# Values in matmuls of 128 patches: a change of lanes in a gated convolution before a GRU scan

## The chip, the cores and the metric

The kernel runs on one core of one Trainium2 chip. The metric is the device time of one execution in microseconds. The engines are TensorE (PE, with its weight loads as PEld), VectorE (DVE), ScalarE (ACT), GpSimd (POOL) and SyncE (SP, which only issues DMAs here). All tensors are float32.

## The reference

Two layers, each with a residual and a group norm in front. Only layer 0 bears on the change. Its input is x, 4 images of 64 channels, 256 x 256 pixels.

```python
hidden = jnp.einsum('bchw,oc->bohw', x, w1)                 # 64 -> 384 channels
hidden = jax.lax.conv_general_dilated(hidden, w_dw, ...)    # 3 x 3, each channel by itself
q, k, v = jnp.split(hidden, 3, axis=1)                      # 128 channels each
qf = jnp.fft.rfft2(_to_patches(q))                          # patches of 8 x 8 pixels
kf = jnp.fft.rfft2(_to_patches(k))
out = jnp.fft.irfft2(qf * kf, s=(P, P))
...
mu = out.mean(axis=1, keepdims=True)                        # over the 128 channels, per pixel
var = out.var(axis=1, keepdims=True)
out = (out - mu) / jnp.sqrt(var + 1e-05) * ln_w[None, :, None, None] + ln_b[None, :, None, None]
out = v * out
return jnp.einsum('bchw,oc->bohw', out, w_out)              # 128 -> 64 channels
```

Layer 1 is a scan of a GRU cell over the 256 columns of the result.

## The kernel before

**Blocks.** Layer 0 runs over NBLK = 32 blocks, each of 128 patches (NP = 128, in two halves of NJ = 64) with all channels. The patches come with a halo, as 100 numbers (10 x 10). In a block:

- Chunk 0, 1 and 2: `pointwise` (line 358) for 16 units of 4 patches in each half. A unit is 8 matmuls into two banks of PSUM, and one copy into `h`, which holds 100 halo pixels on its lanes, and 128 channels by 128 patches along each lane. Most copies are ScalarE's; those of a few units are VectorE's (the last argument). Chunk 0 and 1 bring the first and the second half of q and k, chunk 2 brings v.
- `circular` (line 404), after chunk 0 and again after chunk 1: for sp = 0 to 3, `transform` multiplies `h` by matrices that hold the 3 x 3 taps and the Fourier transform (streamed from DRAM as `t`), ScalarE copies q, VectorE multiplies k by q twice (`products`), POOL adds (`crossed`). `inverse` (line 419) transforms a pair back, 24 matmuls, and ScalarE copies the result into `z`. Four pairs give the 128 channels. An inverse is put off in `pending` and issued by `flush`.
- After chunk 2: `project` for the second half of the block before, then `values` (line 441): for k = 0 to 7, 16 channels each, 32 matmuls with the taps alone, and `keep_values`, which copies to `v`.

**Layout.** `z` and `v` are [128, NJ, E]: the lane is the half of the patches and the pixel (2 x 64), and along it lie 64 patches by 128 channels. The order of the channels is `channel_of`'s.

**The norm and what follows** is a generator, `layer_norm` (line 460), and each call of `go()` issues its next step on VectorE. Its steps in order: statistics of channels 0 to 63 (32 `bn_stats`, in four steps, beside circular(n, 1)), of channels 64 to 127 (16 + 16, after units 6 and 7 of chunk 2), a step with the small instructions on mean and variance and the first of eight passes over `z` (subtract the mean or multiply by the reciprocal deviation, 32 channels at a time), the seven other passes, then eight transposes in blocks of 32 x 32, of `z` and `v` in turn. After them the channels lie on lanes. `gated` (line 515) scales and shifts `z` on ScalarE and multiplies `v` by it on POOL, for 32 channels a call. `project` (line 539) is 32 matmuls of 512 columns into four banks: each row tile of the array has its own bank. `add_residual` (line 556) adds x from the four banks with four VectorE instructions, `leave` takes statistics and writes `x1`.

**Order.** Every instruction goes through `InOrder`, so each engine runs its own in the program's order. The norm of block n runs while block n + 1 is computed: the passes and transposes beside its chunk 0, `gated` beside circular(n + 1, 0), `project` and `add_residual` of u = 0 after unit 11 of chunk 1 and of u = 1 after chunk 2. The last stands like this (lines 685 to 689):

```python
            po = project(n - 1, 1) if n else None
            go(1)
            if n:
                add_residual(1, po, xr[1])
            go(3)
```

**Banks.** PSUM is one ring of eight banks, and `psum` (line 283) hands them out in the order of the calls; a call for four starts at bank 0 or 4. Who is given a bank again waits until its last reader is done.

```python
        def psum(banks=2):
            at = place[0] + (-place[0]) % banks
            place[0] = (at + banks) % 8
            return ring[:, at % 8 : at % 8 + banks]
```

Of the kernel before, what the change touches and what calls it, by code (L numbers as in the profile page):

```python
# [9 lines left out]
F32 = mybir.dt.float32  # L10
# [7 lines left out]
E = 2 * C  # L18
P = 128
# [16 lines left out]
def channel_of(f):  # L36

    pair, rest = divmod(f, 32)
    c, r = divmod(rest, 8)
    t, s = divmod(r, 4)  # L40
    return (2 * pair + t) * 16 + 4 * s + c
# [121 lines left out]
def tile_conv_then_gru(  # L163
# [47 lines left out]
    with tc.tile_pool(name="xa", bufs=5) as xa, tc.tile_pool(name="sta", bufs=1) as sta, tc.tile_pool(  # L211
# [55 lines left out]
        wo_sb = const.tile([P, 4, C], F32, tag="wo", name="wo_sb")  # L267
        nc.sync.dma_start(wo_sb, w_out.rearrange("a f b c -> (a f) b c"))
        ln_sb = const.tile([P, 2, 4], F32, tag="ln", name="ln_sb")
# [6 lines left out]
    with layer0 as s:  # L276
# [13 lines left out]
        z = big.tile([P, NJ, E], F32, tag="z", name="z")  # L290
        v = big.tile([P, NJ, E], F32, tag="v", name="v")
        wk = big.tile([P, 7, 1024], F32, tag="wk", name="wk")
        lnst = big.tile([P, 512], F32, tag="lnst", name="lnst")
        seen = big.tile([P, 1024], F32, tag="seen", name="seen")
        moments = big.tile([P, 2, NJ], F32, tag="moments", name="moments")
# [39 lines left out]
        def unit_of(n, chunk, unit, vector):  # L335
# [5 lines left out]
            for j in range(4):  # L341
# [12 lines left out]
                h.rearrange("p c (g n) -> p g c n", g=2)[:, :, c0:c1, unit * 4 : unit * 4 + 4],  # L354
# [64 lines left out]
        def inverse(n, pair):  # L419

            pz = psum(4)
            for i in range(2):
                slot = PAIRS[pair % 2][i]
                both = wk[:, slot : slot + 2].rearrange("p t (r s g n) -> p r g t s n", r=2, g=2, n=NJ)
                for part in range(2 - i):
                    for g in range(2):
                        for c in range(4):
                            at = slice(32 * c, 32 * c + 32)
                            nc.tensor.matmul(
                                pz[g * 64 : g * 64 + 64, c].rearrange("p (t s n) -> p t s n", t=2, n=NJ),  # L430
                                lhsT=g_sb[at, part, i, :],
                                rhs=both[at, part, g],
                                start=i == part == 0,
                                stop=i == 1,
                                tile_position=(32 * c, g * 64),
                            )
            nc.scalar.copy(
                z[:, :, 32 * pair : 32 * pair + 32], pz.rearrange("p c (f n) -> p n (c f)", n=NJ)
            )

        def values(n, k, pv):

            m = matrix(n, 2, k)
            for f in range(16):
                for g in range(2):
                    nc.tensor.matmul(
                        pv[g * 64 : g * 64 + 64, f // 8, (f % 8) * NJ : (f % 8) * NJ + NJ],
                        lhsT=m[0:HALO, f, :],
                        rhs=h[:, 16 * k + f, g * NJ : g * NJ + NJ],
                        start=True,  # L450
                        stop=True,
                        tile_position=(0, g * 64),
                    )

        def keep_values(k, count, pv):
            nc.scalar.copy(
                v[:, :, 16 * k : 16 * (k + count)], pv.rearrange("p x (f n) -> p n (x f)", n=NJ)
            )

        def layer_norm(n):  # L460

            st = lnst[:, 0:384].rearrange("p (a i k) -> p a i k", a=2, k=6)
            spare = lnst[:, 384:512].rearrange("p (a n) -> p a n", a=2)
            mean, rstd = moments[:, 0], moments[:, 1]

            def statistics(a, p0, p1):

                for p in range(p0, p1):
                    nc.vector.bn_stats(
                        st[:, a, p, :],  # L470
                        z[:, 2 * p : 2 * p + 2, 64 * a : 64 * a + 64].rearrange("p n f -> p f n"),
                    )

            for i in range(4):
                statistics(0, 8 * i, 8 * i + 8)
                yield
            statistics(1, 0, 16)
            yield
            statistics(1, 16, NJ // 2)
            yield  # L480
            by = st.rearrange("p a i (e k) -> p a (i e) k", e=2)
            d, total = spare[:, 0], spare[:, 1]
            nc.vector.tensor_tensor(d, by[:, 0, :, 1], by[:, 1, :, 1], ALU.subtract)
            nc.vector.tensor_tensor(total, by[:, 0, :, 2], by[:, 1, :, 2], ALU.add)
            nc.vector.tensor_tensor(d, d, d, ALU.mult)
            nc.vector.scalar_tensor_tensor(d, d, 32.0, total, ALU.mult, ALU.add)
            nc.scalar.activation(rstd, d, AF.Sqrt, bias=eps, scale=1.0 / E)
            nc.vector.tensor_tensor(mean, by[:, 0, :, 1], by[:, 1, :, 1], ALU.add)
            nc.vector.tensor_scalar(mean, mean, 0.5, None, ALU.mult)
            nc.vector.reciprocal(rstd, rstd)  # L490

            def scaled(i):
                f = slice(32 * i, 32 * i + 32)
                for part, what in ((mean, ALU.subtract), (rstd, ALU.mult)):
                    nc.vector.tensor_tensor(
                        z[:, :, f],
                        z[:, :, f],
                        part.rearrange("p (n x) -> p n x", x=1).to_broadcast([P, NJ, 32]),
# [4 lines left out]
            def turned(of, i):  # L503
                chunk = of[:, :, 32 * i : 32 * i + 32]
                nc.vector.transpose(chunk, chunk)

            for i in range(4):
                yield from scaled(i)
            for i in range(4):
                turned(z, i)  # L510
                yield
                turned(v, i)
                yield

        def gated(n, i):
            f = slice(32 * i, 32 * i + 32)
            nc.scalar.activation(
                z[:, :, f],
                z[:, :, f],
                AF.Identity,  # L520
                bias=ln_sb[:, 1, i : i + 1],
                scale=ln_sb[:, 0, i : i + 1],
            )
            nc.gpsimd.tensor_tensor(v[:, :, f], v[:, :, f], z[:, :, f], ALU.mult)
# [14 lines left out]
        def project(n, u):  # L539
            po = psum(4)  # L540
# [415 lines left out]
```

## Time and profile before

| what | value |
|---|---|
| runs of the kernel before | 5211.36, 5244.66 and 5206.85 us, median 5211.36 |
| the profiled execution | 5232.48 us, span of the core 5230.5 us |
| granted TensorE clock, mean | 0.991 |
| moved by DMA | 785.06 MB, mean 150 GB/s |
| `values`: 16384 matmul records of 64 columns | 509.6 us busy, 35.3 us of waits before them |
| `bn_stats` of the norm | 2048, 416.6 us busy |
| passes over z | 256, 2278 ns each |
| transposes of z and of v | 128 each, 2293 and 2288 ns |
| ScalarE's copies of z, and of v | 128 at 1866 ns, 160 at 1521 ns in the mean |
| POOL's product of `gated` | 128 at 4556 ns |

One matmul of the program is two records in the profile[...]. In the rows of the profile the columns are: start and length in microseconds, engine, line, operation, what it writes and reads, and how many; in brackets the idle time of the engine before it, and what ended that. Nearly all rows have line 157, the helper that keeps the order, so a row is told by its tiles: `psring` is the ring of PSUM banks, `psring<-h,t` with 64 columns are the values, `psring<-v,wo_sb` is `project`. In the windows a row gives, for each engine, busy time and count, then the granted clock of TensorE (1.00 is full speed), the DMA share, and GB/s.

### The profile page before, as it was taken

How to read it: one execution, taken by the hardware profiler on the slowest of the kernel's cores; microseconds unless marked ns; L12 is line 12 of the kernel's file. 1: busy time of each engine (PE TensorE's matmuls, PEld its weight loads, DVE VectorE, ACT ScalarE, POOL GpSimd, SP SyncE). 2: the span in 40 equal slices, each digit the busy share in tenths (PEclk: the TensorE clock that was granted, in tenths of full speed). 3: DMA queues.
4: the chain of work that ended last, by engine and by line, in shares of the span. 5: the costliest groups of instructions: out<-in, count | busy, mean ns of one | idle time of the engine just before them, and what ended most of it. 6: DMA issues, size and time to landing. Idle time of an engine off the chain costs nothing.

```text
span 5230.5 us, 284031 instructions
## 1 busy us (share of the span) xinstructions
PE 4908.2 (94%) x131172; PEld 4285.8 (82%) x131172; DVE 4046.2 (77%) x7000; ACT 3325.4 (64%) x4253; POOL 1729.3 (33%) x1723
## 2 busy tenths in 40 slices
PE   4999999999999999999999999999699999999999
PEld 3888888788888888878887888888489999999998
DVE  4678888878788877888887777887677777777777
ACT  3666666666666666666666666676366666666665
POOL 0233332333323343333333323224243333333332
PEclk9999999999999999999999999999899999999999
DMA  7566766666666666666666556556443333333332
GB/s 264 147 168 173 187 175 167 169 174 175 176 183 179 168 170 170 174 182 174 171 171 158 148 157 167 163 150 162 108 118 99 98 98 100 99 97 98 99 99 66
DMA packets 421206, 785.06 MB, mean 150 GB/s; under 512 B 32604, under 2 KB 295552, under 8 KB 417632
## 3 DMA queue, kind: packets, MB, share of 16 engines
q1 hardware_dynamic: 366464, 533.76, 37.9%
q0 software_dynamic: 53264, 232.55, 15.2%
q8 instruction: 1027, 16.83, 1.4%
q14 instruction: 163, 1.34, 0.1%
q10 hardware_dynamic: 288, 0.58, 0.0%
HBM read 622.72 MB, written 144.05 MB: 147 GB/s over the span
## 4 chain that ended last, share of the span: by engine, by line
PE 82%; issue 6%; ACT 5%; DVE 4%; DMA 3%; POOL 1%; ACTq 0%; POOLq 0%; SPq 0%; DVEq 0%
PE psring L157 56%; PE pshz L157 8%; PE pshr L157 8%; PE psni L157 6%; DMA t<-t_all 2%; PE pshn L157 2%; ACT v L157 1%; DVE wk L157 1%; ACT z L157 1%; ACT xq L157 1%; DVE z L157 1%; DMA seen<-in_x 1%; DVE bn L157 0%; POOL v L157 0%; ACT h L157 0%
## 5 line engine op out<-in xcount | busy, mean ns | idle before, releaser
L157 PEld LDWEIGHTS psring<-h,t 100*32 100x32 f32 x49152 | 1387.6, 120 | 250.7 <-issue 198.0
L157 PE MATMUL psring<-h,t 100*32 100x128 f32 x49152 | 1468.2, 257 | 98.4 <-issue 63.2
L157 PEld LDWEIGHTS psring<-w_sb,xq 64*100 64x100 f32 x24576 | 1366.9, 164 | 126.4 <-issue 92.7
L157 PE MATMUL psring<-w_sb,xq 64*100 64x128 f32 x24576 | 1424.7, 272 | 37.3 <-issue 24.2
L157 ACT COPY h<-psring 100x1024 f32<-100x1024 f32 (+2 forms) x1371 | 1234.4, 988 | 332.3 <-PE psring L157 331.1
L157 DVE TENSOR_TENSOR wk<-psring,wk 128x1024 f32<-128x1024 f32 (+1 forms) x768 | 759.3, 1037 | 475.4 <-PE psring L157 333.6
L157 POOL TENSOR_TENSOR v<-v,z 128x2048 f32<-128x2048 f32 x128 | 582.6, 4556 | 667.1 <-DVE wk L157 603.6
L157 DVE TENSOR_TENSOR z<-z,moments 128x2048 f32<-128x2048 f32 x256 | 577.9, 2278 | 2.3
L157 ACT ACTIVATE z<-pshz,b_rz 128x288 f32<-128x288 f32 (+7 forms) x510 | 242.1, 475 | 467.2 <-PE pshz L157 467.2
L157 POOL TENSOR_TENSOR wk<-wk 128x1024 f32<-128x1024 f32 x128 | 303.2, 2369 | 619.9 <-DVE wk L157 605.4
L157 POOL TENSOR_TENSOR raw<-raw,st 128x512 f32<-128x512 f32 x256 | 303.1, 1184 | 535.6 <-DVE st L157 401.7
L157 ACT COPY z<-psring 128x2048 f32<-128x2048 f32 x128 | 238.9, 1866 | 358.8 <-PE psring L157 269.0
L157 PE MATMUL pshr<-st,wi 64*64 64x144 f32 (+7 forms) x12240 | 435.4, 270 | 23.9 <-DVE st L157 13.9
L157 PE MATMUL pshz<-st,wi 64*64 64x144 f32 (+7 forms) x12240 | 435.9, 270 | 10.7 <-issue 9.1
L157 PE MATMUL psni<-st,wi 64*64 64x144 f32 (+7 forms) x12240 | 433.1, 270 | 6.0 <-issue 2.3
L157 DVE COPY h<-psring 100x1024 f32<-100x1024 f32 x229 | 277.1, 1213 | 198.7 <-PE psring L157 185.0
L157 ACT COPY wk<-psring 128x1024 f32<-128x1024 f32 x256 | 259.4, 1013 | 251.8 <-PE psring L157 221.1
L157 DVE SCALAR_TENSOR_TENSOR g<-z,xn 128x288 f32<-128x288 f32 (+7 forms) x510 | 225.7, 443 | 249.9 <-ACT z L157 247.3
L157 DVE BATCH_NORM_STATS2 lnst<-z 128x6 f32<-128x128 f32 x2048 | 416.6, 281 | 0.0
L157 PEld LDWEIGHTS psni<-st,wi 64*64 64x64 f32 x12240 | 366.5, 133 | 47.8 <-issue 10.5
L157 ACT COPY v<-psring 128x2048 f32<-128x2048 f32 (+1 forms) x160 | 243.3, 1521 | 253.9 <-PE psring L157 253.9
L157 PE MATMUL psring<-wk,g_sb 32*64 32x512 f32 x6144 | 383.5, 602 | 18.4 <-issue 15.4
(96 smaller groups left out, 6733.7 us busy)
## 6 DMA issues: line engine op xcount, KB each, us to landing
t<-t_all SPq DMA_DIRECT2D x768, 400.0 KB
xq<-in_xh POOLq DMA_DIRECT2D x128, 800.0 KB, 5.9
wk<-in_x SPq DMA_DIRECT2D x256, 256.0 KB
x<-wk POOLq DMA_DIRECT2D x256, 256.0 KB, 5.4
seen<-in_x POOLq DMA_DIRECT2D x96, 512.0 KB, 7.4
raw<-x SPq DMA_DIRECT2D x128, 256.0 KB
raw<-x SPq DMA_DIRECT2D x256, 128.0 KB
out<-raw SPq DMA_DIRECT2D x128, 256.0 KB
```

Of the source, the lines that this page charges most:

```text
L157: return self.tc.keep_in_program_order(got(*args, **kwargs))
```

## The change

The lanes of `z` and `v` become channel parity and pixel: `z` and `v` are [128, NP, C], with 128 patches by 64 channels along each lane, and two neighbouring channels stand on the two halves of the lanes.

- `values` issues 16 matmuls of 128 columns for each k instead of 32 of 64. `inverse` issues the same 24 matmuls, with the parity in place of the half. The copies to `z` and `v` are as large as before; a pair's copy writes 16 of 64 channels for all 128 patches.
- `layer_norm`: each lane has half of a pixel's channels. So there are 128 `bn_stats` of 64 columns for 64 of 128 columns, the small instructions are on 128 patches and not 64, and the two halves of the lanes are joined by a copy across and four more instructions.
- Passes, transposes and `gated` go over 64 patches by 32 channels; `gated(i)` has channels b and half u from i = 2b + u, where it had four groups of channels.
- `project(u, a)` is half of the former `project`, 16 matmuls. Two row tiles of the array now write one bank, so the order of row tiles and banks changes between a = 0 and a = 1, and a copy of one column on ScalarE stands between: it waits for the first half's last matmuls, and the second half waits for it.
- Places: gated 3 goes from circular(n, 0) to behind unit 3 of chunk 1; project(0, 0) behind unit 12, project(0, 1) and its add_residual behind unit 13, `leave` behind unit 15 (before: 11, 11, 13); project(1, 0) behind unit 14 of chunk 2, project(1, 1) behind unit 15. The copy of unit 11 of chunk 1 is VectorE's in place of that of unit 12.

```diff
-        z = big.tile([P, NJ, E], F32, tag="z", name="z")
-        v = big.tile([P, NJ, E], F32, tag="v", name="v")
+        z = big.tile([P, NP, C], F32, tag="z", name="z")
+        v = big.tile([P, NP, C], F32, tag="v", name="v")
...
             nc.scalar.copy(
-                z[:, :, 32 * pair : 32 * pair + 32], pz.rearrange("p c (f n) -> p n (c f)", n=NJ)
+                z[:, :, 16 * pair : 16 * pair + 16], pz.rearrange("p c (s n) -> p n (c s)", n=NP)
             )
...
             m = matrix(n, 2, k)
-            for f in range(16):
-                for g in range(2):
+            for j in range(8):
+                for e in range(2):
                     nc.tensor.matmul(
-                        pv[g * 64 : g * 64 + 64, f // 8, (f % 8) * NJ : (f % 8) * NJ + NJ],
-                        lhsT=m[0:HALO, f, :],
-                        rhs=h[:, 16 * k + f, g * NJ : g * NJ + NJ],
+                        pv[e * 64 : e * 64 + 64, j // 4, (j % 4) * NP : (j % 4) * NP + NP],
+                        lhsT=m[0:HALO, 2 * j + e, :],
+                        rhs=h[:, 16 * k + 2 * j + e, :],
...
             for i in range(4):
-                statistics(0, 8 * i, 8 * i + 8)
+                statistics(0, 16 * i, 16 * i + 16)
+                if i == 3:
+                    nc.vector.tensor_copy(own, by[:, :, 1:3])
                 yield
-            statistics(1, 0, 16)
-            yield
-            statistics(1, 16, NJ // 2)
-            yield
+            for i in range(2):
+                statistics(1, 32 * i, 32 * i + 32)
+                yield
...
+            nc.vector.tensor_tensor(own, own, by[:, :, 1:3], ALU.add)
+            nc.vector.scalar_tensor_tensor(d, d, -2.0, own[:, :, 0], ALU.mult, ALU.add)
+            nc.vector.tensor_tensor(d, d, d, ALU.mult)
+            nc.vector.scalar_tensor_tensor(rstd, d, 16.0, rstd, ALU.mult, ALU.add)
+            for e in range(2):
+                nc.vector.tensor_copy(other[64 * e : 64 * e + 64], own[64 - 64 * e : 128 - 64 * e])
+            nc.vector.tensor_tensor(apart, mean, other[:, :, 0], ALU.subtract)
+            nc.vector.tensor_tensor(own, own, other, ALU.add)
+            nc.vector.tensor_tensor(apart, apart, apart, ALU.mult)
+            nc.vector.scalar_tensor_tensor(rstd, apart, 8.0, rstd, ALU.mult, ALU.add)
+            nc.scalar.activation(rstd, rstd, AF.Sqrt, bias=eps, scale=1.0 / E)
+            nc.vector.tensor_scalar(mean, mean, 0.25, None, ALU.mult)
             nc.vector.reciprocal(rstd, rstd)
...
+        def project(u, a, po=None, first=[]):
+            po = psum(4) if po is None else po
+            y = v.rearrange("p n (b k) -> p b n k", k=32)
+            for b in range(2):
+                for e in range(2):
+                    for ph in range(2):
+                        for s in range(2):
+                            r, g = 2 * e + ph, a ^ e
+                            n0 = 64 * u + 32 * g + 16 * s
+                            i = nc.tensor.matmul(
+                                po[s * 64 : s * 64 + 64, 2 * g + ph].rearrange("p (n k) -> p n k", k=32),
+                                lhsT=wo_sb[32 * r : 32 * r + 32, b, :],
+                                rhs=y[32 * r : 32 * r + 32, b, n0 : n0 + 16],
+                                start=a == b == 0,
+                                stop=a == b == 1,
+                                tile_position=(32 * r, s * 64),
+                            )
+                            if a == 0 and b == 1:
+                                first.append(i)
+                            if a == 1 and b == 0 and first:
+                                behind(i, first.pop())
+            if a == 0:
+                turn = nc.scalar.copy(tick, eps)
+                while first:
+                    behind(turn, first.pop())
+                first.append(turn)
+            return po
...
-                if n and sp == 3:
-                    gated(n - 1, sp)
...
-                pointwise(n, 1, unit, unit in (7, 12))
-                if n and unit == 11:
-                    add_residual(0, project(n - 1, 0), xr[0])
+                pointwise(n, 1, unit, unit in (7, 11))
+                if n and unit == 3:
+                    gated(n - 1, 3)
+                if n and unit == 12:
+                    po = project(0, 0)
                 if n and unit == 13:
+                    add_residual(0, project(0, 1, po), xr[0])
+                if n and unit == 15:
                     leave(n - 1, 0, xr[0])
...
+                if n and unit == 14:
+                    po = project(1, 0)
                 if unit % 4 == 3 and n + 1 < NBLK:
                     load(n + 1, unit // 4)
-            po = project(n - 1, 1) if n else None
+            if n:
+                project(1, 1, po)
             go(1)
             if n:
                 add_residual(1, po, xr[1])
```

## The prediction

> **What bounds the kernel now.** I read the engine totals first, then the chain that ended last, then the timeline of one block of layer 0 engine by engine.
>
> ```profile
> PE 4908.2 (94%) x131172; PEld 4285.8 (82%) x131172; DVE 4046.2 (77%) x7000; ACT 3325.4 (64%) x4253; POOL 1729.3 (33%) x1723
> PE 82%; issue 6%; ACT 5%; DVE 4%; DMA 3%; POOL 1%; ACTq 0%; POOLq 0%; SPq 0%; DVEq 0%
> ```
>
> TensorE is busy 94% of the span and 82% of the chain. So what this change is worth is read from TensorE: each microsecond it works less or waits more counts, and work of the others counts only where TensorE waits for it. Layer 1 (from about 3790 us on) is untouched. Layer 0 runs 32 blocks; by the starts of their first matmuls, blocks 2 to 30 take 113.3 us each in the mean (108.5 to 120.4). All numbers below are of block 12 (1462.7 to 1576.3 us) where nothing else is said. Its end on TensorE:
>
> ```profile
> 1546.73 8.98 PE L157 MATMUL psring<-w_sb,xq 64*100 64x128 f32 x160 [0.16 <-ACT z L157]
> 1555.64 3.69 PE L157 MATMUL psring<-v,wo_sb 32*64 32x512 f32 x64
> 1559.26 11.38 PE L157 MATMUL psring<-h,t 100*64 100x64 f32 x371
> 1572.02 4.31 PE L157 MATMUL psring<-h,t 100*64 100x64 f32 x141 [1.37 <-issue]
> ```
>
> The last pointwise units of chunk 2, project(1), then the values, without a pause between. And VectorE meanwhile:
>
> ```profile
> 1549.11 6.37 DVE L157 BATCH_NORM_STATS2 lnst<-z 128x6 f32<-128x128 f32 x32
> 1555.83 1.22 DVE L157 COPY h<-psring 100x1024 f32<-100x1024 f32 x1 [0.35 <-PE psring L157]
> 1556.97 0.53 DVE L157 TENSOR_TENSOR lnst<-lnst 128x64 f32<-128x64 f32 x3
> 1557.53 0.22 DVE L157 SCALAR_TENSOR_TENSOR lnst<-lnst 128x64 f32<-128x64 f32 x1
> ...
> 1558.17 0.55 DVE L157 RECIPROCAL moments<-moments 128x64 f32<-128x64 f32 x1
> 1558.64 2.23 DVE L157 TENSOR_TENSOR z<-z,moments 128x2048 f32<-128x2048 f32 x1
> 1560.79 2.47 DVE L157 TENSOR_TENSOR wk<-psring,wk 128x512 f32<-128x512 f32 x4
> ```
>
> The reader is to see the order of this queue: statistics, the copy of unit 15, the norm's small instructions, the first pass over z, and only then add_residual(1), which empties the four banks of project(1). It ends at 1563.26, four microseconds after the values began. That is harmless now: project(1) sits in banks 4-7, and values k = 0 and 1 take banks 0-3.
>
> **The change, part by part** (per block; blocks 1 to 31 have all of it).
>
> *Values.* 512 records of 64 columns become 256 of 128. Unstalled, 141 records take 4.31 us, 30.6 ns each, 15.7 us in all. 128 columns over two tiles of the array: 8.98/160 = 56.1 ns (the pointwise row), so 14.4 us: -1.3. The Trainium skill, "TensorE: Matmul & The Clock Gate", section "Wait — 56ns, not 53.3ns?", gives about 2.5 ns of fixed cost for a matmul; 256 records less would by that be worth only 0.6 us. I take the rows. ScalarE takes part back: its copies of v and normalisations of xq start when k = 1 is done (1563.26) and the copy of k = 3 and 4, which frees the banks of k = 6, starts 5.92 us later (1569.18) and takes 1.86. With k = 0 and 1 in 3.6 us that is 3.6 + 5.9 + 1.9 = 11.4, where TensorE would be ready at 10.8. So -0.7 (-1.3 to 0).
>
> *Banks.* The ring hands out banks in order of calls. project(1, 0) is now called one unit earlier, before unit 15. By the allocation rule in psum() it gets banks 0-3, unit 15 gets 4-5, and the next call for four banks, values k = 0, rounds up to 0-3 again: those of project(1). So the values now wait for add_residual(1), bank by bank, and that stands in VectorE's queue behind the norm and the first pass over z. This is the largest term.
>
> *The norm on VectorE.* bn_stats of 128 columns follow each other at 199 ns (6.37/32), of 512 at about 0.6 us (2.46 us for four); that gives 0.13 us for 64. The 64 in units 6 and 7 take 8.3 us, +1.9, about what unit 15 comes later (half of project, 1.85), so they hide. Behind unit 15's copy the small instructions take 1.67 us now (1556.97 to 1558.64). Then: five of 128 columns at about 0.23 (0.19 for 64, from 0.56 us for three, and 1.04 ns a column), 1.15; two of 256 at 0.39, 0.78; two copies across half the lanes at 0.25 to 0.39, 0.6; from the last one over ScalarE's square root to the reciprocal 0.64 now, 0.76; the reciprocal 0.47 now, and 64 columns more at 6.3 ns (553 ns for 64 columns, 177 for 4), 0.87. Sum 4.2 us.
>
> *The gate.* From TensorE's end of unit 15: 1.33 to the small instructions, 4.2 for them, 2.15 for the first pass (1558.64 to 1560.79), 0.7 for the first add: the values start after 8.4 us. From the same point project and nothing else took 3.62. Now half of project lies ahead of unit 15: 1.85 + 8.4 - 3.62 = +6.6 (5.5 to 7.5, as the small instructions take 3.2 to 5 us). The second half of project covers 1.85 of the 8.4, so TensorE stands idle for 6.5 us.
>
> *The clock.* A long pause costs more than itself here. At 253.00 TensorE paused for 3.12 us; after it:
>
> ```profile
> 253.00:256.20 3.20, 0.08 (x3) 0.08 (x2) 0.00 (x0) 0.90 (x1) 3.20 (x1) 1.00 0.99 169
> 256.20:259.60 3.40, 3.40 (x32) 3.40 (x34) 0.00 (x0) 1.18 (x2) 3.40 (x2) 0.50 0.29 100
> 259.60:263.00 3.40, 3.40 (x67) 3.40 (x64) 2.42 (x3) 2.50 (x3) 0.13 (x1) 1.00 0.00 0
> ```
>
> (busy time and count of PE first, the granted clock third from the end: 0.50, and 32 matmuls where the next 3.4 us hold 67.) So 1.7 us are lost. The same page, section "HAM oscillation — how this bites in real kernels", puts it as a rule that TensorE must not idle for more than about 3.4 us, and describes a loop that pays at every turn. The trace has too few such pauses for "at every turn"; without the rule this term could be 0, with it 1.7 to 3.4 (two stretches). I take +1.7.
>
> *z's copy in circular(n, 0).* A pair's copy now writes 16 channels of all 128 patches, so the first overlaps what gated 0 and gated 1 read; before it met gated 0 alone. POOL and ScalarE in the next block:
>
> ```profile
> 1605.32 4.60 POOL L157 TENSOR_TENSOR v<-v,z 128x2048 f32<-128x2048 f32 x1
> ...
> 1606.68 1.86 ACT L157 COPY z<-psring 128x2048 f32<-128x2048 f32 x1 [2.42 <-PE psring L157]
> 1608.60 1.01 ACT L157 COPY wk<-psring 128x1024 f32<-128x1024 f32 x1
> ```
>
> gated 1 ends at 1609.92, so z's copy slips by 3.2 us (median over the blocks 3.1), and behind it on ScalarE the copy of q for sp = 3, for which VectorE's products wait, and the copies of h. Moving gated 3 to unit 3 of chunk 1 takes 2.1 us of ScalarE out of that queue, and puts it where two later units may wait for copies. Following the banks: unit 0 of chunk 1 waits about 1.1 us for z's banks, unit 3 about 0.8 for the late products. +2.0 (0 to 2.5).
>
> *Statistics in circular(n, 1).* 4 x 16 instead of 4 x 8 at 0.13: +0.5 us at each step of VectorE, where it has 0.5 to 2.8 us of idle time; TensorE waited there for crossed and products already (0.91, 0.46). +0.5 (0 to 1.2).
>
> *project in two halves with a copy of one column on ScalarE between.* Same 64 records. The copy needs some 0.3 us (the sqrt of 64 columns takes 0.35), a pointwise unit of 0.9 us lies between the halves: hidden in both places; without that unit it would be about 0.5. Unit 15 of chunk 1 waits for the first two adds, +0.4, where before the inverse waited 0.2. project(0) no longer needs gated 3: TensorE waited 2.1 us in all for this row in layer 0, so nothing. The inverse has the same 24 matmuls: nothing. DMAs are as many; leave(0) is two units later, but its writes to x1 wait for the adds, not for this place.
>
> *What becomes free.* From the first matmul of the values to the first of the next block it is 16.67 us in the mean of blocks 2 to 30, where 15.72 is the least: TensorE lost 0.95, partly to weights that had not landed; a pause in front lets them land: -0.5. VectorE was late for units 3 and 9 of chunk 0 by about 0.4; TensorE now comes later: -0.4.
>
> Sum: -0.7 + 6.6 + 1.7 + 2.0 + 0.5 + 0.2 - 0.9 = +9.4 us, 31 times 291 us. The profiled execution took 5232, the median of the runs is 5211, 21 lower; blocks are as many in both, so the sum goes onto the median: about 5500.
>
> **The rivals.**
>
> *Gate without the rest.* If the clock holds, z's copy is hidden and the small instructions take 3.2 us, 4.6 a block remain: about 5355. Against it: the pause is still over 3.4 us.
>
> *VectorE as the bound, no gate.* From 1549 to 1615 VectorE idles for 2.5 us; 1.9 of statistics and 2.5 of small instructions make it longer by 2 us: 31 x 2 = 62, about 5275. It holds only if the values don't wait for project's banks.
>
> *Faster.* If the chain on VectorE were done in 1.9 us after unit 15 (it takes 1.33 before its first small instruction), the values would start as before and shorten: 31 x 0.7 to 1.3, 5170 to 5190. It decides by where add_residual(1) stands against the first pass over z, and the order is written down: behind it.
>
> *The change does less than it says:* TensorE could need as long for 128 columns as for two times 64. That would add 1.3 x 31 = 40 to any of these.
>
> **How the numbers follow.** The gate with clock and z's copy: 0.84, 5500, by its own bounds 5390 to 5610. The gate alone: 0.08. VectorE's bound: 0.03. No net difference: 0.02. Faster: 0.03. 1% of 5211 is 52 us, about what a measurement tells from no change; VectorE's bound lies on its edge and counts half for each side. Slower 0.94, same 0.03, faster 0.03. The range goes from 5375, which takes in part of the gate alone, to 5605.
>
> **What would show it.** Right: in the PE timeline a pause of 5 to 7 us before the values in each of the blocks 1 to 31, released by DVE wk; the values' row at x8192, about 450 us without the pauses; granted clock near 0.97 with a stretch of 0.5 after each pause; the first z copy of a block waiting for POOL v. Wrong: no pause ahead of the values (then the banks are not as I count them), a pause without a drop of the clock (then 5440), ScalarE's z copy not later than before (5430).

## The result, and the profile after

The changed kernel takes 5626.01 us in the median of 6 runs (5619.83 to 5633.22); the kernel before, run beside it, 5217.79 (6 runs). The ratio is 1.0769, with a 95% interval from 1.0746 to 1.0792. The forecast was 5500, with a range from 5375 to 5605: slower, as said, but by 408 us where the sum had 291, and 21 us above the top of the range.

The profiled execution took 5633.22 us, its span is 5631.4, its mean TensorE clock 0.966 (before 0.991). First the engine totals and the chain that ended last, from its page:

```profile
PE 5032.4 (89%) x122980; PEld 4370.6 (78%) x122980; DVE 4273.6 (76%) x9240; ACT 3347.3 (59%) x4317; POOL 1730.6 (31%) x1723
PE 65%; DVE 11%; ACT 8%; issue 7%; DMA 5%; POOL 3%; POOLq 0%; DVEq 0%; ACTq 0%; SPq 0%
```

TensorE had 82% of the chain and has 65% now; VectorE has 11% of it and ScalarE 8%. Who waits for whom is in the summary of waits (total us, times, longest), first of the kernel before:

```profile
PE psring L157 <- DVE wk L157: 2.9, 5, 1.2
```

and of the changed one:

```profile
PE psring L156 <- DVE wk L156: 237.5, 63, 7.4
```

`DVE wk` is VectorE writing `wk`, which is the add of the residual or a product of `circular`. The pauses ahead of the values, 31 of 7.0 us, make some 217 of the 237.5. The timeline of block 12 at its end, TensorE (start, length, what, count, in brackets the idle time before and its releaser):

```profile
1702.18 6.36 PE L156 MATMUL psring<-w_sb,xq 64*100 64x128 f32 x112 [0.96 <-DVE h L156]
1708.47 2.45 PE L156 MATMUL psring<-v,wo_sb 32*64 32x512 f32 x32
1710.86 1.12 PE L156 MATMUL psring<-w_sb,xq 64*100 64x128 f32 x16
1711.91 1.97 PE L156 MATMUL psring<-v,wo_sb 32*64 32x512 f32 x32
1720.89 7.76 PE L156 MATMUL psring<-h,t 100*64 100x128 f32 x96 [7.01 <-DVE wk L156]
1728.87 5.46 PE L156 MATMUL psring<-h,t 100*64 100x128 f32 x96 [0.22 <-ACT v L156]
```

and VectorE in the same stretch:

```profile
1699.36 1.29 DVE L156 BATCH_NORM_STATS2 bn<-seen 128x6 f32<-128x512 f32 x2 [4.75 <-DMA seen<-in_x]
...
1703.17 8.26 DVE L156 BATCH_NORM_STATS2 lnst<-z 128x6 f32<-128x64 f32 x64
1712.10 1.23 DVE L156 COPY h<-psring 100x1024 f32<-100x1024 f32 x1 [0.66 <-PE psring L156]
1713.24 0.42 DVE L156 TENSOR_TENSOR lnst<-lnst 128x256 f32<-128x256 f32 x1
1713.69 0.33 DVE L156 SCALAR_TENSOR_TENSOR lnst<-lnst 128x128 f32<-128x128 f32 x1
1714.05 0.33 DVE L156 TENSOR_TENSOR lnst<-lnst 128x128 f32<-128x128 f32 x1
...
1717.15 0.95 DVE L156 RECIPROCAL lnst<-lnst 128x128 f32<-128x128 f32 x1 [0.34 <-ACT lnst L156]
1718.02 2.23 DVE L156 TENSOR_TENSOR z<-z,lnst 128x2048 f32<-128x2048 f32 x1
1720.16 2.47 DVE L156 TENSOR_TENSOR wk<-psring,wk 128x512 f32<-128x512 f32 x4
```

and, in circular(n, 0) of the same block, POOL's product of gated 1 and ScalarE's first copy to z:

```profile
1640.11 4.54 POOL L156 TENSOR_TENSOR v<-v,z 128x2048 f32<-128x2048 f32 x1
1644.68 1.87 ACT L156 COPY z<-psring 128x2048 f32<-128x2048 f32 x1 [5.62 <-POOL v L156]
```

The reader is to see five things. The pause of 7.01 us stands where the prediction put it, and ends when the first add has read the first bank of project(1) (1720.16 plus 0.7). The first 96 records of the values take 7.76 us, the next 96 take 5.46: that is the half clock after the pause, as e3 below shows. The first half of project(1) takes 2.45, the second 1.97. VectorE stood 4.75 us at a count of the next image, waiting for its DMA. And z's copy stood 5.62 us, until gated 1 was done on POOL (2.42, for TensorE, before the change).

For the whole run, here are the stages of a block: microseconds between the first matmuls of stages, taken from the starts in the trace, as means of blocks 2 to 30. The last three columns are kernels of the experiments.

| stage | before | changed | e1 | e8 | e9 |
|---|---|---|---|---|---|
| chunk 0 | 15.28 | 14.87 | 19.24 | 15.15 | 15.15 |
| circular(n, 0) | 19.00 | 20.08 | 19.83 | 20.26 | 22.35 |
| chunk 1 with project(0) | 18.65 | 21.01 | 20.98 | 21.03 | 21.07 |
| circular(n, 1), 4 units of chunk 2, inverse | 28.10 | 28.09 | 28.22 | 28.48 | 28.33 |
| 12 units of chunk 2, project(1), pause | 15.62 | 24.97 | 18.43 | 18.45 | 17.14 |
| values | 16.67 | 17.74 | 17.93 | 17.89 | 15.67 |
| a block | 113.3 | 126.8 | 124.6 | 121.3 | 119.7 |

So the change costs 13.5 us a block, not 9.4. What the values save is there, but hidden under the clock; two stages bring what the prediction did not have: chunk 1 with project(0), and chunk 2.

### The profile page after: what moved, and what is told of

It reads as the page before. It is cut to its first block, busy times and chain, and to the rows that moved or that the text cites. A ratio compares the mean times of both kernels' runs of the same rounds, so it can differ in the third digit from the quotient of the medians.

```text
span 5631.4 us, 269678 instructions
## 1 busy us (share of the span) xinstructions
PE 5032.4 (89%) x122980; PEld 4370.6 (78%) x122980; DVE 4273.6 (76%) x9240; ACT 3347.3 (59%) x4317; POOL 1730.6 (31%) x1723
## 4 chain that ended last, share of the span: by engine, by line
PE 65%; DVE 11%; ACT 8%; issue 7%; DMA 5%; POOL 3%; POOLq 0%; DVEq 0%; ACTq 0%; SPq 0%
PE psring L156 41%; PE pshz L156 8%; PE pshr L156 8%; PE psni L156 6%; DVE wk L156 4%; DVE lnst L156 3%; POOL v L156 3%; DMA seen<-in_x 3%; ACT v L156 2%; PE pshn L156 2%; DVE z L156 2%; ACT z L156 2%; DMA t<-t_all 2%; ACT h L156 2%; ACT xq L156 1%
## 5 line engine op out<-in xcount | busy, mean ns | idle before, releaser
L156 PE MATMUL psring<-h,t 100*32 100x128 f32 x40960 | 1503.9, 279 | 310.6 <-DVE wk L156 219.6
L156 PE MATMUL psring<-w_sb,xq 64*100 64x128 f32 x24576 | 1475.4, 275 | 114.2 <-DVE h L156 32.3
L156 DVE TENSOR_TENSOR z<-z,lnst 128x2048 f32<-128x2048 f32 x256 | 578.1, 2279 | 2.3
L156 DVE BATCH_NORM_STATS2 lnst<-z 128x6 f32<-128x64 f32 x4096 | 539.2, 216 | 0.0
L156 PE MATMUL pshr<-st,wi 64*64 64x144 f32 (+7 forms) x12240 | 480.3, 270 | 24.5 <-DVE st L156 13.7
L156 PE MATMUL pshz<-st,wi 64*64 64x144 f32 (+7 forms) x12240 | 481.8, 270 | 7.4 <-issue 6.2
L156 PE MATMUL psni<-st,wi 64*64 64x144 f32 (+7 forms) x12240 | 478.5, 270 | 4.5 <-issue 3.1
L156 PEld LDWEIGHTS psni<-st,wi 64*64 64x64 f32 x12240 | 424.0, 133 | 16.5 <-issue 12.2
L156 PEld LDWEIGHTS pshr<-st,wi 64*64 64x64 f32 x12240 | 396.3, 133 | 39.2 <-issue 20.3
L156 PEld LDWEIGHTS pshz<-st,wi 64*64 64x64 f32 x12240 | 399.4, 133 | 19.9 <-issue 18.7
```

Source lines behind the costliest of these rows:

```text
L156: return self.tc.keep_in_program_order(got(*args, **kwargs))
```

## The experiments

Each kernel is the changed one with the edit shown, where nothing else is said. The kernel before took 5227 us beside e1 to e4, 5228 beside e5 to e7 and b1, 5222 beside e8 and e9, and 5155 beside the last two: those are compared by ratio.

**e1, the adds ahead of the norm.** It takes away what the values wait for, without touching a bank.

```diff
-            go(1)
             if n:
                 add_residual(1, po, xr[1])
-            go(3)
+            go(4)
```

> The changed kernel, with add_residual(1) issued ahead of the norm's small instructions and the first pass, so that the values' banks come free as soon as project(1, 1) is done. Theory (the values wait for add_residual behind the norm): the pause of 7.0 us before the values shrinks to under 1.5 us in each block, and the stretches of half clock behind it go. How much of it reaches the end: if TensorE then sets the pace again, 6.3 us and 2.3 us of clock in 31 blocks, 5626 - 267 = about 5360. If VectorE's queue is the next bound (its work from the copy of unit 15 to the first products is some 3.5 us longer than before and was nearly without idle time there), TensorE waits later, in chunk 0, and only 4 to 5 us a block are won: 5470 to 5500, the granted clock at 0.98 or above. Rival (the pause is due to something else, such as the weights or the turn between the halves): the pause stays, 5600 or more.

Measured: 5581.05 (5575.48 to 5583.26), ratio 1.0672 [1.063, 1.0714]. That lies above what the theory gave and below its rival. The pause is gone (project(1) to values 9.00 to 2.79 us), but only 45 us came back: chunk 0 of the next block went from 14.87 to 19.24. In the waits of this kernel stand, new,

```profile
PE psring L156 <- DVE h L156: 106.0, 44, 3.9
PE psring L156 <- ACT v L156: 69.3, 62, 2.1
```

The first are units 3 and 9 of chunk 0, which VectorE copies: it stands behind three passes over z there. The second is mostly ScalarE's first copy of v, behind the square root, which now comes later since VectorE adds first, while the values come earlier. So the pause had covered the lateness of VectorE. It was not the end of the cost.

**e2, the values in other banks.** The order stays, and only who inherits project(1)'s banks changes.

```diff
+            place[0] = 4
             for k in range(8):
```

> The changed kernel, with the ring set so that the first values take banks 4-7 and not those of project(1); the order on VectorE is as it was. Theory: values k = 0 and 1 start right behind project (pause under 0.5 us), and the wait for add_residual comes at k = 2, as about 3 us; with a shorter pause the clock drops less. With TensorE as the pace-setter 7 to 8 us a block are won, 5380 to 5410; with VectorE as the next bound 4 to 5 us, 5470 to 5500, about the same as with the adds first. Rival (the banks do not matter): 5600 or more and the pause of 7 us unchanged.

Measured: 5536.52 (5518.84 to 5554.46), ratio 1.0586 [1.0542, 1.0629], the best of all single edits, but above both of its theory's sums. TensorE in block 12:

```profile
1677.39 1.97 PE L156 MATMUL psring<-v,wo_sb 32*64 32x512 f32 x32
1679.29 3.71 PE L156 MATMUL psring<-h,t 100*64 100x128 f32 x64
1686.42 9.70 PE L156 MATMUL psring<-h,t 100*64 100x128 f32 x128 [3.41 <-DVE wk L156]
```

k = 0 and 1 (64 records) start at once. The wait for the same adds stands at k = 2 now, which takes project(1)'s banks; 3.41 us of it are left, and the records behind it still run at a lowered clock (9.70 for 128, where 3.71 for 64 makes 7.4). Only the numbers of the banks change, so the wait is one of inherited banks. The trace holds a second case of it: in blocks 7, 15 and 23 of this kernel it is 8.98 us from project(1, 1) to the values, as without the edit, and 1.90 in all others of blocks 1 to 30. These three start the norm of the next image, which calls `psum` twice ahead of project(1, 0). By the count of calls that moves project(1) to banks 4-7, which are the ones that the edit gives to the values.

**e3, the pause filled.** Ten matmuls without use behind project(1, 1), so that TensorE waits as long but doesn't stand still.

```diff
             if n:
                 project(1, 1, po)
+                for _ in range(10):
+                    nc.tensor.matmul(ring[0:64, 6, 0:HID], lhsT=g_sb[:, 0, 0, :], rhs=w1_sb, start=True, stop=True)
```

> The changed kernel, with ten matmuls of 384 columns that nobody reads put behind project(1, 1), some 6.5 us of TensorE work in the pause. If half clock after the pause costs what the trace suggests (values take 17.7 us where 15.1 to 15.7 would do), the values shorten by 2 us and more: 5626 - 31 x 2.2 = about 5558, the granted clock back near 0.99. Rival (the values are long for another reason, ScalarE's copies or weights that come late): no change, 5615 to 5640, although the clock is back.

Measured: 5563.83 (5541.97 to 5583.15), ratio 1.0637 [1.0589, 1.0684], clock 0.989, near the theory's 5558.

```profile
1692.22 6.66 PE L156 MATMUL psring<-w_sb,g_sb 128*64 128x384 f32 x20
1699.33 5.46 PE L156 MATMUL psring<-h,t 100*64 100x128 f32 x96 [0.44 <-DVE wk L156]
```

The values start as late as with the pause, but their first 96 records take 5.46 us instead of 7.76; the stage falls from 17.74 to 15.43, by 2.3 us, which is what a pause costs by the clock. And 15.43 against 16.67 before is what the wide matmuls save with the feed of weights: 1.24.

**e4, no product for gated 1.** It leaves out a quarter of the products v x z (POOL's for i = 1).

```diff
-            nc.gpsimd.tensor_tensor(v[:, n, f], v[:, n, f], z[:, n, f], ALU.mult)
+            if i != 1:
+                nc.gpsimd.tensor_tensor(v[:, n, f], v[:, n, f], z[:, n, f], ALU.mult)
```

> The changed kernel without POOL's product of gated 1 (a quarter of v is left unmultiplied, so the output is not the reference's). Theory (z's first copy waits for gated 1, and ScalarE's queue behind it): the copy starts about 3 us sooner, chunk 1 starts 1.0 us sooner and loses 1.0 us less on the way to project: 2.0 us a block, 5626 - 64 = about 5560. Rival (the place of gated 3 among the units of chunk 1 is what costs): no more than 0.5 us a block, 5610 or more. POOL has 4.5 us less to do in this kernel, which could win a little elsewhere too.

Measured: 5582.16 (5565.66 to 5596.16), ratio 1.0672 [1.0629, 1.0714]: 44 us, 1.4 a block, between the theory's 2.0 and its rival's 0.5. The last transform of circular(n, 0) falls from 5.01 to 3.96, before the change it was 4.02. That part is z's copy. Of the other, in chunk 1 (12 units took 11.11 before, a unit is 0.87, and 13 take 13.07), a third came back: 12.75.

**e5, the halves of project further from the copies they may wait for.**

```diff
-                if n and unit == 12:
+                if n and unit == 11:
                     po = project(0, 0)
-                if n and unit == 13:
+                if n and unit == 12:
                     add_residual(0, project(0, 1, po), xr[0])
...
-                if n and unit == 14:
+                if n and unit == 13:
                     po = project(1, 0)
```

> The changed kernel with the first halves of the two projections one unit earlier, the second halves where the units' copies are one older (project(0, 0) behind unit 11, project(0, 1) behind unit 12, project(1, 0) behind unit 13), so that the banks of each first half were last used by units whose copies are a unit older. Theory (the halves cost time because they wait for copies of the units just before them): the first halves take 1.9 us instead of 2.4 and the unit behind each 0.9 instead of 1.05, that is 1.1 to 1.7 us of a block, 5575 to 5590 us. Rival (TensorE loses the time itself whenever it changes between units and halves of a projection): first halves stay at 2.3 to 2.4 us, 5615 to 5635 us.

Measured: 5607.79 (5593.95 to 5611.18), ratio 1.0733 [1.0707, 1.0759], between the two. The first halves take 1.90 each, as the theory says, so the rival falls. But at project(0) nothing is saved: the three units behind the second half now take 3.78, with waits of 0.5 us at two of them. In block 12 of this kernel, VectorE and TensorE:

```profile
1651.22 2.48 DVE L156 TENSOR_TENSOR wk<-psring,wk 128x512 f32<-128x512 f32 x4 [3.71 <-PE psring L156]
```

```profile
1649.12 1.97 PE L156 MATMUL psring<-v,wo_sb 32*64 32x512 f32 x32
1651.03 3.85 PE L156 MATMUL psring<-w_sb,xq 64*100 64x128 f32 x48
```

The adds run until 1653.70, and only one unit behind the second half has banks that are not theirs: the unit between the halves has used the other pair. Before, two units ran while VectorE added.

**e6, the last count of a block later.**

```diff
-                if more and unit == 2:
+                if more and unit == 5:
                     count(n, 12)
...
-                if image and unit in (4, 8, 12):
+                if image and unit in (7, 10, 13):
```

> The changed kernel with the last count of a block (count(n, 12), two bn_stats of a piece that a DMA brings) behind unit 5 of chunk 2 instead of unit 2, and the steps of the next image's norm behind units 7, 10 and 13. Theory (VectorE stands at that count until the DMA has landed, its copies of units 4 and 6 come late, and TensorE waits for banks): the 11 units of chunk 2 take 10.1 us instead of 12.6 in the 23 blocks that count, 1.5 to 2.4 us each, 5560 to 5595 us. Rival (the wait is covered, and the units are late for the statistics of the norm in front of it): no change, 5615 to 5635 us.

Measured: 5598.39 (5592.17 to 5615.41), ratio 1.0725 [1.0698, 1.0752], 3 us above what the theory gave, and against the rival. In the changed kernel the waits had

```profile
DVE bn L156 <- DMA seen<-in_x: 83.3, 22, 6.1
```

and here that row reads

```profile
DVE bn L156 <- DMA seen<-in_x: 13.0, 10, 3.1
```

The 11 units fall from 12.59 to 11.47 us. The blocks that begin a new image (7, 15, 23) still take 18 to 19 us here, and the others 10.1 to 12.9 (10.1 to 15.4 with the early count). **b1** makes the same edit in the kernel before:

> The kernel before the change with count(n, 12) behind unit 5 of chunk 2 and the steps of the next image's norm behind units 7, 10 and 13. Theory (the same wait of VectorE for the DMA of that count holds chunk 2 of the kernel before by some 0.9 us of a block, by the length of its 12 units): up to 25 us less, 5190 to 5205 us where the kernel before has 5215. Rival (the units are long there for another reason): within 8 us of the kernel before.

Measured: 5229.93 in 22 runs against 5227.74 in 27, ratio 1.0009 [0.9996, 1.0022]. The kernel before has this row

```profile
DVE bn L157 <- DMA seen<-in_x: 60.1, 24, 4.6
```

which here falls to 6.7 us in 7 waits, and nothing is gained: there the wait was covered or came back at another place. What covered it no run shows.

**e7, e1 without the joining of the lanes.** It leaves out that two lanes' mean and variance are combined, and normalizes over half the channels.

```diff
-            for e in range(2):
-                nc.vector.tensor_copy(other[64 * e : 64 * e + 64], own[64 - 64 * e : 128 - 64 * e])
-            nc.vector.tensor_tensor(apart, mean, other[:, :, 0], ALU.subtract)
-            nc.vector.tensor_tensor(own, own, other, ALU.add)
-            nc.vector.tensor_tensor(apart, apart, apart, ALU.mult)
-            nc.vector.scalar_tensor_tensor(rstd, apart, 8.0, rstd, ALU.mult, ALU.add)
```

> The kernel with add_residual(1) first, with the joining of the two lanes left out of the norm (the two copies of own into other, and the four instructions that combine mean and variance, some 2.1 us of VectorE in a block), so that it normalizes over half of the channels. Theory (with the gate gone, VectorE's work of a block sets the pace): 2.1 us less in 31 blocks than with the joining, 5581 - 65 = about 5516 us. Rival (VectorE has slack there, TensorE or ScalarE sets the pace): 5570 to 5585 us as with the joining.

Measured: 5518.59 (5512.27 to 5538.49), ratio 1.0579 [1.0547, 1.0611]. The time is the theory's, within 3 us, and it would have been easy to stop there: VectorE is the bound. But the stages say where it came from: the values fell from 17.93 to 15.41 and chunk 0 rose to 20.03. Its waits:

```profile
PE psring L156 <- DVE h L156: 128.2, 47, 3.6
...
PE psring L156 <- ACT v L156: 16.4, 55, 0.4
```

VectorE is felt at two points, the copy of v behind the square root and the copies of units 3 and 9. A sum of work that sets the pace, and two points at which it is waited for, give the same number here. The next run separates them.

**e8, e1 with units 3 and 9 of chunk 0 on ScalarE.**

```diff
-                    pointwise(n, 0, unit, unit in (3, 9) if norm else unit % 2)
+                    pointwise(n, 0, unit, False if norm else unit % 2)
```

> The kernel with add_residual(1) first (5581 us), and units 3 and 9 of chunk 0 copied by ScalarE instead of VectorE in every block but the first. Theory (with the gate gone, VectorE is late by several us when chunk 0 begins, and TensorE feels it only through these two copies): chunk 0 takes about 16.5 us instead of 19.24 (16 copies of 1.0 us on ScalarE), VectorE has 2.5 us less to do, in all 2 to 2.7 us of a block: 5495 to 5520 us. Rival (ScalarE has no room for two more copies, or VectorE's lateness only moves on into the two lanes' products and gated): 5565 to 5590 us.

Measured: 5469.82 (5457.57 to 5479.35), ratio 1.0471 [1.044, 1.0501]: 111 us less than e1 (105 by the ratios), more than VectorE's work fell (2.5 us x 31 = 76), more than the theory allowed. The row of e1 with 106.0 us now reads

```profile
PE psring L156 <- DVE h L156: 26.8, 16, 4.0
```

So VectorE's sum of work was not the bound; the order of its queue was, at two copies.

**e9, the cures together:** e8, with the norm behind the first copy of v, the late count, and project(1, 0) behind unit 13.

```diff
-            go(4)
             for k in range(8):
...
                     keep_values(k - 1, 2, pv)
+                    if k == 1:
+                        go(4)
```

> The cures that the single runs priced, together: add_residual(1) first, units 3 and 9 of chunk 0 on ScalarE, the norm's chain behind the first copy of v (so that this copy doesn't stand behind the square root on ScalarE), count(n, 12) behind unit 5 with the image's steps behind units 7, 10 and 13, and project(1, 0) behind unit 13. Theory (the costs are separate and add up): from e8 by theory (about 5507) less 1.1 us for the count, 0.4 for the half, and 1 to 2.4 for the values, in 31 blocks: 5385 to 5430 us, still 3 to 4% over the kernel before, since z's copies behind gated, the second halves' adds and VectorE's longer statistics stay. Rival (VectorE's sum of work is the bound, so that what is taken from one stage comes back in another): 5490 to 5580 us.

Measured: 5426.35 (5418.1 to 5435.95), ratio 1.0392 [1.0357, 1.0426], clock 0.988. That is within what the theory gave (5385 to 5430), near its upper end, since circular(n, 0) grew by 2.1 us: POOL stood idle before crossed, because VectorE's products were late, and then had gated 1 and z's copy behind it.

```profile
1552.33 4.61 POOL L156 TENSOR_TENSOR v<-v,z 128x2048 f32<-128x2048 f32 x1 [15.44 <-ACT z L156]
1560.90 2.36 POOL L156 TENSOR_TENSOR wk<-wk 128x1024 f32<-128x1024 f32 x1 [3.96 <-DVE wk L156]
1563.21 4.57 POOL L156 TENSOR_TENSOR v<-v,z 128x2048 f32<-128x2048 f32 x1
```

**e10 and e11.** e10 is e9 with POOL's product of gated 1 ahead of crossed(0). e11 is e10 with both halves of project(0) behind unit 12.

```diff
-                if sp == 1 or (a and sp == 3):
+                if a and sp % 2:
                     crossed(sp // 2)
...
                     gated(n - 1, sp)
+                if sp == 1:
+                    crossed(0)
                 go()
```

> The kernel with the cures together (5426 us), and POOL's product of gated 1 ahead of crossed(0) in circular(n, 0), where POOL stood idle for some 4 us until VectorE's products were done. Theory (z's first copy waits for the product of gated 1, and with it the copies behind it on ScalarE): that product ends about 3 us earlier, chunk 1 begins 1 to 1.5 us earlier, and its units wait up to 1 us less for banks: 1.0 to 2.5 us of a block, 5350 to 5395 us. Rival (crossed(0), now behind the product, is late instead, and the inverse waits for it as long): 5415 to 5440 us.

> The kernel with POOL's product of gated 1 ahead, and both halves of project(0) behind unit 12, with no unit between them. Theory (the unit between takes one of the two pairs of banks that are free beside the four of project, so a unit behind the second half waits for the adds; without it two units run while VectorE adds, and the second half waits for ScalarE's copy of one column): the project and the units around it take 0.3 to 0.8 us less of a block, 10 to 25 us less than with the unit between. Rival (the wait for the copy of one column costs as much as the unit behind gains): within 8 us of the kernel with the unit between.

Measured: e10 5328.31 (5311.71 to 5329.03), ratio 1.0346 [1.0315, 1.0377]; e11 5319.72 (5309.97 to 5325.33), ratio 1.0327 [1.0298, 1.0356]; the kernel before took 5155.23 beside both. By its ratio e10 would take about 5403 where e9 takes 5426, so just short of the theory; the intervals of the two ratios overlap. The stages are clearer: circular(n, 0) and chunk 1 together fall from 43.42 to 41.78 us. z's copy waits for nothing of POOL's any more (last transform 5.21 to 3.63), but crossed(0) is later and so is the inverse (5.31 to 6.13): both sides of the expectation have a share. What chunk 1 still waits, with z's copy on time, is in block 12 of e10 for ScalarE, which does gated 3 behind unit 3 now (no run puts gated 3 back):

```profile
1542.76 7.24 PE L156 MATMUL psring<-w_sb,xq 64*100 64x128 f32 x128
1550.63 4.70 PE L156 MATMUL psring<-w_sb,xq 64*100 64x128 f32 x80 [0.63 <-ACT h L156]
```

For e11, the two halves take 4.69 with the wait for ScalarE's copy between, the three units 2.80, and the inverse waits 0.34 for the adds; from the first half to the end of the inverse that is 10.59 against 10.70. The stages speak for the rival: the place of this unit makes 0.1 us. The 8.6 us between the two medians lie between the rival's 8 and the theory's 10, within the intervals, and decide nothing.

No kernel with the new lanes beats the kernel before. In e11 a block still takes 4.3 us more: 2.4 in circular(n, 0), 1.3 in chunk 1 and 1.6 in the stage of project(1), while the values take 1.1 less. No run puts project(1, 0) back behind unit 15, where by the count of calls the values would not get its banks.

## Why the prediction fell short

By its own steps, in microseconds a block (what the stages and the runs show, against the sum's terms):

| step | said | shown | by |
|---|---|---|---|
| values and their weights | -0.7 and -0.5 | -1.24 | e3, values at full clock |
| gate | +6.6 | +7.2 | 9.00 from project(1, 1) to the values, where the path had 8.4 |
| clock | +1.7 | +2.3 | e3 |
| z's copy behind gated 1 | +2.0 | +2.1 | last transform +1.0, chunk 1's units +1.1 |
| statistics in circular(n, 1) | +0.5 | 0 | stage 28.10 to 28.09 |
| project in two halves | +0.2 | +1.9 | +1.3 at project(0), +0.6 at project(1) |
| units 3 and 9 | -0.4 | -0.4 | chunk 0 |
| count of the next image | none | +1.5 | the 11 units of chunk 2, 12.59; 12 units took 12.00, one is 0.87 |
| sum | +9.4 | +13.4 | measured +13.5 |

**What was right.** The gate, its cause and its place: the values inherit project(1)'s banks, and the adds stand behind the norm and the first pass. e2 shows it by the banks alone, e1 by the order. z's copy was right in size, and e4 and e10 show the cause for the half of it that lies in circular(n, 0). Of the rest, in chunk 1, about half goes with z's copy (13.13 to 12.49 in e10) and half stays, by the trace behind gated 3 on ScalarE; the prediction had counted the two as one term. The values' gain was right.

**The step that failed** is the one on project's halves, "hidden in both places" with +0.2 for all of it. Two of its claims broke. The first halves take 2.40 and 2.33 instead of 1.9: they wait for copies of units just before them, which e5 shows by moving them. And "unit 15 waits for the first two adds, +0.4, where before the inverse waited 0.2" was too little: the unit between the halves takes one of the two free pairs of banks, so one unit behind the second half runs while VectorE adds, where before two did. At project(0) the two halves take 4.30 us where project took 3.73, and the three units behind the first half 3.63 (with the waits in them) where three of the former four took 2.93. At project(1) e5 won 0.8 us of the stage (24.97 to 24.17); at project(0) e5 and e11 move the cost and don't remove it. With +1.9 the sum is 1.7 higher, 53 us.

**The step that was missing** is VectorE's wait for the next image's piece. It stood in the trace of before (60.1 us over 24 waits), and b1 shows that it costs nothing there. The prediction has no term for it, and gives no reason for that. In the changed kernel it holds back the copies of units 4 and 6; e6 recovered 1.1 of the 1.5 us. Why VectorE waits longer for the piece now (83.3 us) wasn't tried; the transfers take as long as before (median 7.4 us to landing before, 7.6 now).

These two, 1.7 and 1.5 us in 31 blocks, are 99 us: without them the time would lie near 5527 and within the range. Every other term that had bounds came out within them.

**Two sizes were low.** The small instructions take 4.78 us (1713.24 to 1718.02) instead of 4.2. Those on 128 columns start 0.36 us apart, where the prediction added 1.04 ns a column to 0.19 and had 0.23 (its own figures make 0.25). And the clock: one stretch at half speed was taken, but e3 shows 2.3 us. The rule that was weighed there (the Trainium skill, "TensorE: Matmul & The Clock Gate", section "HAM oscillation — how this bites in real kernels"), that TensorE must not idle for more than about 3.4 us, decided rightly that a loop pays for such a pause at every turn: around each of the 31 pauses the trace has a stretch of 6.8 or 10.2 us at half clock. As a limit its figure is a little high here: the prediction's own example, a pause of 3.12 us, was followed by half clock too.

**The rivals.** Of "VectorE as the bound" one half was seen in e1, when the gate was gone: the kernel gained 45 us and not the 267 that TensorE's own time would have given. But e8 shows two copies in its queue, and not its sum of work. The prediction could have named this: its own line "VectorE was late for units 3 and 9 by about 0.4; TensorE now comes later" treats the pause as a cover.

## What to carry to other kernels

When buffers come from a ring by order of calls, write down for each call whose buffer it inherits, before and after: here one call moved by one place made the largest term. A pause that is taken away gives back only what nobody else was late by; look for the next waits under it, and try moving two copies to another engine before calling an engine the bound. A run whose time is just what a theory gave can still be right for another reason; the stages tell.

## What the runs showed of the hardware

The granted clock, in windows of block 12 (busy time and count of PE first, the granted clock third from the end), shows how long a pause of 7 us is paid for:

```profile
1717.20:1720.60 3.40, 0.00 (x0) 0.00 (x0) 3.40 (x3) 0.00 (x0) 0.00 (x0) 0.74 0.00 0
1720.60:1724.00 3.40, 3.11 (x30) 3.11 (x32) 3.40 (x5) 0.00 (x0) 0.00 (x0) 0.50 0.00 0
1724.00:1727.40 3.40, 3.40 (x52) 3.40 (x50) 3.37 (x3) 0.45 (x1) 0.00 (x0) 0.76 0.35 96
1727.40:1730.80 3.40, 3.18 (x60) 2.94 (x58) 3.40 (x4) 3.40 (x3) 0.12 (x1) 1.00 0.62 178
```

The clock falls while TensorE still stands, and stays at half for some 5 us after it started: 30 and 52 records where 60 fit. Over the run, all but three stretches at half clock lasted 3.4, 6.8 or 10.2 us (18, 23 and 11 of them); 20 of the 6.8 and all 11 of the 10.2 lie around the pauses. The 3.41 us left in e2 were enough too: in its windows the clock is 0.50 for the 3.4 us after the pause and 0.80 for the next. And short VectorE instructions of the norm follow each other at 0.36 us on 128 columns, one of 256 is followed after 0.45, and those on 64 before the change at 0.19; no run here tells why 128 is so near to 256.
